# The attention mask of the last group: matmuls on TensorE, or products on VectorE and GpSimd

## The chip, the core and the metric

The kernel runs on one core of one Trainium2 chip. The metric is the device time of one launch in microseconds. Three runs of the kernel before have a median of 3718.45 us (3712.51 to 3718.55).

## What is computed

The input is 32 sequences of 256 tokens with 256 features. A gated state-space block (convolution, layernorm, a scan over the tokens, a gate) is followed by two layers of windowed attention with a feed-forward part; the result is added to the input. What matters here is the attention of one layer:

```
qkv = shift_token(x) @ wqkv                      # 8 heads of 64
q, k = l2norm, scale, rotary of q and k
sim  = q * 8 @ k^T                               # windows of 128, each with the window before it
mask = (i < j) | (i > j + WINDOW) | (j == -1)    # i: query token, j: key token
attn = softmax(where(mask, -max, sim))
x = x + (attn @ v) @ wo
...
h = layernorm(shift_token(x)) @ w1 + b1          # the feed-forward part: a * gelu(g), @ w2 + b2
```

With 256 tokens there are two windows. A key of the first window is seen by queries of the first window from its own position on, and by queries of the second window up to its own position; a key of the second window by queries of the second window from its own position on.

## The kernel before

The 32 sequences are taken in four groups of eight (`GB`, `NG`). Each group first goes through the state-space block: `group_scan` writes a list of steps by slot, 256 scan steps long (`step`, L703, on VectorE; its inputs scaled by ScalarE, L693; read out by TensorE, L715). The result of a group goes to DRAM and is loaded again, sequence by sequence, by `load_res`. The scan of group g+1 runs beside the attention of group g, so nothing is left of the scan in most of the last group.

The attention works key-major. `Attention.project` (L1137) makes q, k and v of a window (`ps_qkv`, L962); `rotated` applies the rotary tables and the norm on VectorE (L978, L983, L988, L992) and GpSimd (`rot` L986, `rn` L994, `rot` L995); `turn` transposes q and k (L1001), and ScalarE copies them (L1006).

`scores(b, kw, i0, n)` handles the keys of window `kw` for `n` head pairs from `i0` on. For the two heads of a pair it takes a bank of PSUM each, and into each bank goes first the mask: a bf16 matmul of the identity with `mask_t` (L1161), which is 0 where a key may be seen and -32768 elsewhere. The score matmuls (L1168) add to it. ScalarE takes the exponential of a bank into a tile `pT` (L1177), where the masked places become 0. A sequence has three such calls: window 1 with all four pairs, window 0 with pairs 0 and 1, window 0 with pairs 2 and 3. That is 6 mask matmuls of 128x512, 6 exponentials and 6 tiles `pT`.

`sums` adds up `pT` over the keys (`rs`, L1187), first for key window 0, heads of even number before odd, then for key window 1; VectorE inverts the sums (`rinv`, L1195). `values` multiplies with v (`ov`, L1206; copied by ScalarE, L1213). The inverse sums go through DRAM (`rb`), VectorE multiplies them on (`divide`, L1230), and `project_out` (`ps_wo`, L1012) adds the result to the residual on VectorE (L1020).

The feed-forward part has a layernorm: `normalise` transposes both windows into one bank (`tp_h`, L1249), takes their statistics (L1257, L1258, L1260), and takes the root of both windows in one GpSimd instruction (`rstd`, L1262); `apply` (L1270), `spread` (`tp_hn`, L1282, copied by ScalarE, L1288); then six times `widen` (`pa`, L1309; Gelu on ScalarE, L1317) and `product` (`ag`, L1325, on VectorE), then `narrow` (`po_f`, L1337; VectorE, L1348). In the second layer GpSimd adds the kernel's input (L1356).

The order around the change is set in two steps. A table of stages, eight to a sequence, says in which the parts of a sequence are called (`attend`, `feed`, `fetch`), and the parts of three sequences are interleaved so:

```
stage(n, 3, at.scores, b, 0, 0, 2)
stage(n, 2, at.scores, b, 1, 0, HEADS // 2)
stage(n, 5, at.scores, b, 0, 2, 2)
stage(n, 7, at.sums, b)
stage(n, 7, at.values, b)
```

From these calls a scheduler with its own costs makes the order of instructions on each engine; what is wrapped in `keep_in_program_order` it doesn't move. Each engine then works through its own list in order. DMAs of this part are issued on SyncE's queue.

Of the kernel before, what the change touches and what calls it, by code (L numbers as in the profile page):

```python
# [11 lines left out]
BF = mybir.dt.bfloat16  # L12
I32 = mybir.dt.int32
AF = mybir.ActivationFunctionType
ALU = mybir.AluOpType
# [4 lines left out]
P = 128  # L20
# [18 lines left out]
W = 128  # L39
# [13 lines left out]
def bc(ap, axis, n):  # L53

    ap = ap.unsqueeze(axis)
    shape = list(ap.shape)
    shape[axis] = n
    return ap.broadcast_to(shape)
# [15 lines left out]
def kernel(  # L74
# [29 lines left out]
    nc = tc.nc  # L104
    B = xT.shape[2]
    L = wqkv.shape[1]
    NG = B // GB

    const = ctx.enter_context(tc.tile_pool(name="const", bufs=1))
# [53 lines left out]
    for j in range(NJ):  # L163
# [13 lines left out]
    mask_t = const.tile([P, 2 * W], BF, tag="mask_t", name="mask_t")  # L177
    ident_b = const.tile([P, P], BF, tag="ident_b", name="ident_b")
# [7 lines left out]
        out=mask_t[:, W : 2 * W], in_=mask_t[:, W : 2 * W], compare_op=ALU.is_ge,  # L186
        fill=MASKED_LOW, base=0, pattern=[[-1, W]], channel_multiplier=1,
    )

    head_cols = const.tile([P, 2, 32], FP, tag="head_cols", name="head_cols")  # L190
    nc.gpsimd.memset(head_cols, 0.0)
# [27 lines left out]
    def program(ctx, exact):  # L219
# [802 lines left out]
        if exact:  # L1022

            mask = rpool.tile([P, 2 * W], FP, tag="mask", name="mask")
# [102 lines left out]
        class Attention:  # L1127

            def __init__(self, l):
                self.l = l
                self.qkv, self.rot, self.p, self.o = {}, {}, {}, {}

            def project(self, b, w, a):
                if w == 0 and a == 2:
# [16 lines left out]
            def scores(self, b, kw, i0, n):  # L1153


                qT, kT, _ = self.qkv[b]
                nq = S - kw * W
                banks = []
                for r in range(2):
                    sc = ps_w.tile([P, n, nq], FP, tag="w", name="sc")  # L1160
                    nc.tensor.matmul(  # L1161
                        sc, ident_b, bc(mask_t[:, 0:nq], 1, n), start=True, stop=False
                    )
                    banks.append(sc)
                for i in range(n):
                    for r in range(2):
                        rows = slice(r * DH, (r + 1) * DH)
                        nc.tensor.matmul(  # L1168
                            banks[r][:, i, :],
                            kT[rows, i0 + i, kw * W : (kw + 1) * W],  # L1170
                            qT[rows, i0 + i, kw * W :],
                            start=False,
                            stop=(i == n - 1),
                        )
                for r in range(2):
                    p = aw.tile([P, n, nq], FP, tag="pT", name="pT", bufs=6)
                    nc.scalar.activation(p, banks[r], AF.Exp)  # L1177
                    for i in range(n):
                        self.p[b, kw, i0 + i, r] = p[:, i, :]

            def sums(self, b):

                rs = bank(ps_w, "w", "rs")[:, 0:S]
                for kw in range(NW):
                    for r in range(2):
                        for i in range(HEADS // 2):
                            nc.tensor.matmul(  # L1187
                                rs[32 * i : 32 * i + 32, kw * W :],
                                head_cols[:, r],
                                self.p[b, kw, i, r],  # L1190
                                start=(kw == 0 and r == 0),
                                stop=(kw == NW - 1 and r == 1),
                            )
                rinv = aw.tile([P, S], FP, tag="rinv", name="rinv", bufs=1)
                nc.vector.reciprocal(rinv, rs)  # L1195
                self.rinv = rinv
# [190 lines left out]
        seqs = [(g, l, b) for g in range(NG) for l in range(L) for b in range(GB)]  # L1387
        stages = {}

        def stage(n, i, what, *args):  # L1390
            stages.setdefault(ST * n + i, []).append(partial(what, *args))

        def attend(n, at, b, nxt):

            stage(n, 0, at.turn, b, 1)
            stage(n, 3, at.scores, b, 0, 0, 2)
            stage(n, 2, at.scores, b, 1, 0, HEADS // 2)
            stage(n, 5, at.scores, b, 0, 2, 2)
            stage(n, 7, at.sums, b)
            stage(n, 7, at.values, b)  # L1400
            stage(n + 1, 0, at.put_inverse)
            stage(n + 1, 2, at.load_inverse)
            stage(n + 1, 4, at.divide, b)
            stage(n + 1, 6, at.finish, b)
            if nxt is not None:
                for w in range(NW):
                    for i, a in ((0, 2), (1, 0), (1, 1)):
                        stage(n, 3 * w + i, nxt[0].project, nxt[1], w, a)
                stage(n, 6, nxt[0].turn, nxt[1], 0)
# [22 lines left out]
            if l == L - 1 and g < NG - 1:  # L1432
                stage(n + 6, 2, load_res, g + 1, b)

        ats = [Attention(l) for _, l, _ in seqs]

        for n, (g, l, b) in enumerate(seqs):
            nxt = (ats[n + 1], seqs[n + 1][2]) if n + 1 < len(seqs) else None
            attend(n, ats[n], b, nxt)
            feed(n, g, l, b)  # L1440
# [24 lines left out]
        for t in range(max(stages) + 1):  # L1465
# [3 lines left out]
            g, r = divmod(t + 1 + group - reload, group)  # L1469
# [10 lines left out]
    with tc.If(fits > 0) as which:  # L1480
        with ExitStack() as es:
            program(es, False)
    with which.Else():
        with ExitStack() as es:
            program(es, True)
# [81 lines left out]
def _program(ins, out_shape):  # L1567
    import concourse.bacc as _bacc

    nc = _bacc.Bacc("TRN2", target_bir_lowering=False, num_devices=1)  # L1570
    arrays, args = {}, []
    for name, a in ins.items():
        arrays[f"in_{name}_dram"] = a
        args.append(
            nc.dram_tensor(
                f"in_{name}_dram", a.shape, mybir.dt.from_np(a.dtype), kind="ExternalInput"
            ).ap()
        )
    args.append(nc.dram_tensor("out_0_dram", out_shape, FP, kind="ExternalOutput").ap())
    with tile.TileContext(nc) as tc:  # L1580
        kernel(tc, *args)
    return nc, arrays
# [11 lines left out]
```

## Time and profile before

| what | before |
| --- | --- |
| median of three runs | 3718.45 us |
| the profiled execution | 3716.42 us |
| its span (first to last instruction) | 3714.5 us |
| mean granted clock of TensorE | 0.989 |
| busy: TensorE, VectorE, ScalarE, GpSimd | 3594.4, 2671.9, 2161.5, 1775.9 us |
| mask matmuls (L1161) in the whole span | 384, median 379 ns |

The page gives busy time by engine, the same in 40 slices of the span, the chain that ended last, and groups of instructions by line. PE is TensorE, PEld its weight loads, DVE is VectorE, ACT ScalarE, POOL GpSimd, SP SyncE. A row of the timeline has the start, the time to the end of the last instruction of the row, the engine and line, and in brackets the idle time of the engine before it and what ended it. An fp32 matmul stands in the trace as two instructions. Ends of matmuls are modelled, so the distance from one start to the next says more than a duration.

### The profile page before, as it was taken

The page shows a single profiled execution, that of the slowest core. Times are in us where ns is not written, and L with a number is a line of the kernel's source. Part 1 is how long each engine was busy: PE and PEld are TensorE (multiplying, and loading weights), DVE is VectorE, ACT ScalarE, POOL GpSimd, SP SyncE. Part 2 cuts the span into 40 slices and gives each one's busy share as a digit, 9 for nine tenths or more (in the row PEclk, how much of TensorE's full clock was granted, in tenths as well). Part 3 has the DMA queues.
Part 4 walks back from the last instruction along what each step waited for, and adds up shares of the span by engine and source line. Part 5 has one row for each costly group of instructions (what it writes and reads, how often), then busy time and mean ns, then how long its engine had stood idle before and what let it go on. Part 6 is the DMA issues. An engine that isn't in the chain of part 4 may idle for free.

```text
span 3714.5 us, 56989 instructions
## 1 busy us (share of the span) xinstructions
PE 3594.4 (97%) x19900; PEld 2240.4 (60%) x19900; DVE 2671.9 (72%) x5113; ACT 2161.5 (58%) x3689; POOL 1775.9 (48%) x1712
## 2 busy tenths in 40 slices
PE   7999889999999999999999999999999999999999
PEld 4444335666566566666666666666666666666666
DVE  5888889888787877887778777887776444444443
ACT  3666656666666666666666666666666444444442
POOL 4433366445455555554556555554444444433441
PEclk9999999999999999999999999999999999999999
DMA  7777655445454545445454546445453211011101
GB/s 205 203 198 203 185 164 149 130 110 135 121 140 122 150 129 150 125 112 133 110 138 124 140 138 148 126 108 137 106 135 98 60 35 50 12 35 33 30 27 36
DMA packets 469212, 435.79 MB, mean 117 GB/s; under 512 B 228835, under 2 KB 308532, under 8 KB 468788
## 3 DMA queue, kind: packets, MB, share of 16 engines
q1 hardware_dynamic: 384466, 420.05, 41.7%
q10 hardware_dynamic: 84450, 12.01, 2.1%
q8 instruction: 160, 2.62, 0.3%
q14 instruction: 136, 1.11, 0.1%
HBM read 383.70 MB, written 46.66 MB: 116 GB/s over the span
## 4 chain that ended last, share of the span: by engine, by line
PE 66%; DVE 15%; DMA 6%; POOL 5%; ACT 4%; issue 3%; SPq 0%; ACTq 0%; DVEq 0%; POOLq 0%
PE ps_qkv L962 13%; PE pa L1309 13%; PE po_f L1337 8%; DVE h L703 6%; PE y L715 5%; PE ps_wo L1012 4%; DMA xrep<-xnd 4%; PE sc L1168 4%; PE ov L1206 3%; PE ps_out L793 2%; PE ps_in L395 2%; PE tr_qk L1001 2%; ACT xrep L693 2%; DVE acc L485 2%; PE rs L1187 2%
## 5 line engine op out<-in xcount | busy, mean ns | idle before, releaser
L703 DVE CUSTOM_DVE_ANT_0 h<-h,xrep,lim 128x512 f32<-128x512 f32 x1024 | 950.2, 928 | 235.4 <-ACT xrep L693 200.8
L693 ACT ACTIVATE xrep<-xrep,beta 128x512 f32<-128x512 f32 x960 | 673.7, 719 | 342.5 <-DMA xrep<-xnd 252.5
L962 PE MATMUL ps_qkv<-qkv,res 128*128 128x512 f32 x1536 | 724.4, 607 | 18.4 <-DVE ag L1325 8.1
L1309 PE MATMUL pa<-hT,w 128*128 128x256 f32 (+1 forms) x3072 | 688.8, 386 | 1.4 <-ACT hT L1288 0.7
L1309 PEld LDWEIGHTS pa<-hT,w 128*128 128x128 f32 (+1 forms) x3072 | 492.7, 178 | 186.1 <-issue 77.4
L986 POOL TENSOR_TENSOR rot<-rot,swp 128x512 f32<-128x512 f32 x256 | 335.2, 1309 | 505.4 <-DVE swp L983 399.0
L962 PEld LDWEIGHTS ps_qkv<-qkv,res 128*128 128x128 f32 x1536 | 277.8, 191 | 327.9 <-issue 251.1
L994 POOL TENSOR_TENSOR rn<-ss,neg_half 128x8 f32<-128x8 f32 x256 | 459.2, 1794 | 15.2 <-DVE ss L992 5.2
L1325 DVE SCALAR_TENSOR_TENSOR ag<-pa,b_sb,ag 128x256 f32<-128x256 f32 (+1 forms) x448 | 213.4, 476 | 259.8 <-ACT ag L1317 257.3
L1337 PE MATMUL po_f<-ag,w 128*128 128x256 f32 (+1 forms) x1536 | 386.9, 393 | 11.6 <-DVE ag L1325 7.7
L715 PE MATMUL y<-h,ly 128*32 128x512 f32 x2048 | 356.5, 611 | 14.0 <-DVE h L703 13.1
L1337 PEld LDWEIGHTS po_f<-ag,w 128*128 128x128 f32 (+1 forms) x1536 | 272.7, 189 | 119.0 <-issue 52.0
L1262 POOL TENSOR_TENSOR rstd<-ve,neg_half 128x2 f32<-128x2 f32 x64 | 46.3, 723 | 622.3 <-DVE ve L1260 604.0
L995 POOL TENSOR_TENSOR rot<-rot,rn 128x512 f32<-128x512 f32 x256 | 292.4, 1142 | 20.1
L975 ACT ACTIVATE sq<-ps_qkv 128x512 f32<-128x512 f32 x256 | 151.9, 595 | 227.7 <-PE ps_qkv L962 175.7
L1317 ACT ACTIVATE ag<-pa,b_sb 128x256 f32<-128x256 f32 x320 | 150.2, 469 | 202.4 <-PE pa L1309 201.3
L978 DVE TENSOR_TENSOR rot<-ps_qkv,rc_sb 128x512 f32<-128x512 f32 x256 | 174.8, 683 | 82.9 <-ACT sq L975 82.2
L485 DVE SCALAR_TENSOR_TENSOR acc<-xr,wc_sb,acc 128x256 f32<-128x256 f32 x384 | 194.1, 529 | 53.7 <-POOL acc L474 53.2
L1012 PE MATMUL ps_wo<-oT,wo 128*128 128x256 f32 x1024 | 231.8, 379 | 0.2 <-ACT ag L1317 0.2
L1177 ACT ACTIVATE pT<-sc 128x512 f32<-128x512 f32 x384 | 208.5, 596 | 23.9 <-PE sc L1168 22.4
L1168 PE MATMUL sc<-qT,kT 64*128 64x128 f32 (+1 forms) x2048 | 222.0, 346 | 0.0
L1012 PEld LDWEIGHTS ps_wo<-oT,wo 128*128 128x128 f32 x1024 | 194.2, 190 | 28.3 <-ACT ag L1317 1.2
(150 smaller groups left out, 5437.0 us busy)
## 6 DMA issues: line engine op xcount, KB each, us to landing
xrep<-xnd SPq DMA_DIRECT2D x960, 256.0 KB
rb<-inv SPq DMA_DIRECT2D x128, 256.0 KB
xnd<-xn SPq DMA_DIRECT2D x64, 256.0 KB
qkv<-in_wqkv_dram SPq DMA_DIRECT2D x24, 512.0 KB
ahead<-xs_a SPq DMA_DIRECT2D x48, 256.0 KB
xp<-ahead SPq DMA_DIRECT2D x48, 256.0 KB
xd<-xnd SPq DMA_DIRECT2D x192, 64.0 KB
w<-in_w_dram SPq DMA_DIRECT2D x80, 128.0 KB
```

The source lines that it names most:

```text
L485: nc.vector.scalar_tensor_tensor(acc, xr[:, :, k : k + CH], wc_sb[:, ch, k : k + 1], acc, ALU.mult, ALU.add,)
L693: scaled = nc.scalar.activation(bx, ck[c].pop(("bx", t), bx), AF.Copy, scale=ck[c]["beta"][:, t : t + 1])
L703: nc.vector._custom_dve(TENSOR_ADD_SAT, out=h_new, in0=state["h"], in1=bx, s0=ck[c]["lim"][:, 0, t : t + 1], s1=ck[c]["lim"][:, 1, t : t + 1],
L715: nc.tensor.matmul(ck[c]["y", hb][32 * q : 32 * q + 32, :], ly[hb % 2][:, 32 * t : 32 * t + 32], ck[c].pop(("h", hb * TB + t)), start=(i = ...
L962: nc.tensor.matmul(ps, res[b][:, k, t0 : t0 + W], wt["qkv", a][:, k], start=(k == 0), stop=(k == KM - 1),)
L986: nc.gpsimd.tensor_add(rot, rot, swp)
L994: nc.gpsimd.tensor_tensor(rn, ss, neg_half, ALU.pow)
L995: nc.gpsimd.tensor_mul(rot, rot, bc(rn, 2, DH))
L1012: nc.tensor.matmul(po[:, d], wt["wo", 0][:, c, d * P : (d + 1) * P], oT[:, c, :], start=(c == 0), stop=(c == NC_ - 1),)
L1168: nc.tensor.matmul(banks[r][:, i, :], kT[rows, i0 + i, kw * W : (kw + 1) * W], qT[rows, i0 + i, kw * W :], start=False, stop=(i == n - 1),)
L1309: nc.tensor.matmul(pg if x else pa, wt["w1", m][:, k, x], self.h[:, k], start=(k == 0), stop=(k == KM - 1),)
L1337: nc.tensor.matmul(self.po[:, d], wt["w2", 0][r0 : r0 + n, m, d * P : (d + 1) * P], self.ag[m][r0 : r0 + n], start=(m == 0), stop=(m == le ...
```

## The change

In the last group (`g == NG - 1`, both layers) the mask matmuls are left out: each score matmul starts its own part of the bank, and the exponential is taken of the unmasked scores. Afterwards the tiles `pT` are multiplied in place by `mask_1`, which is 1 where a key may be seen and 0 elsewhere. GpSimd does that for the two tiles of key window 1, VectorE for the four of key window 0. `mask_1` is made once in the setup, by one GpSimd comparison of `mask_t`. The products are called at stages 3, 4 and 6 of their sequence, each a stage after its scores, and keep their place in the program's order. The other three groups are as before. The description of the change names the layernorm of both halves together as well: the diff has no line in it, and the kernel before already takes both windows together, as told above.

```diff
+    mask_1 = const.tile([P, 2 * W], BF, tag="mask_1", name="mask_1")
+    nc.gpsimd.tensor_scalar(mask_1, mask_t, -1.0, None, ALU.is_ge)
...
-            def __init__(self, l):
+            def __init__(self, g, l):
                 self.l = l
-                self.qkv, self.rot, self.p, self.o = {}, {}, {}, {}
+
+                self.apart = g == NG - 1
+                self.qkv, self.rot, self.p, self.ps, self.o = {}, {}, {}, {}, {}
...
-                    nc.tensor.matmul(
-                        sc, ident_b, bc(mask_t[:, 0:nq], 1, n), start=True, stop=False
-                    )
+                    if not self.apart:
+                        nc.tensor.matmul(
+                            sc, ident_b, bc(mask_t[:, 0:nq], 1, n), start=True, stop=False
+                        )
...
-                            start=False,
-                            stop=(i == n - 1),
+                            start=self.apart,
+                            stop=self.apart or i == n - 1,
...
                     nc.scalar.activation(p, banks[r], AF.Exp)
+                    self.ps[kw, i0, r] = p
...
+            def mask(self, kw, i0):
+
+                e = nc.gpsimd if kw else nc.vector
+                for r in range(2):
+                    p = self.ps.pop((kw, i0, r))
+                    n, nq = p.shape[1:]
+                    tc.keep_in_program_order(
+                        e.tensor_mul(p, p, bc(mask_1[:, 0:nq], 1, n))
+                    )
...
+            if at.apart:
+                for i, what in ((3, (1, 0)), (4, (0, 0)), (6, (0, 2))):
+                    stage(n, i, at.mask, *what)
...
-        ats = [Attention(l) for _, l, _ in seqs]
+        ats = [Attention(g, l) for g, l, _ in seqs]
```

## The prediction

> **What bounds the kernel now.** I read the page first (engine shares, then the 40 slices), then the table of stages, then the groups of the last stage alone, and last the timelines of TensorE, VectorE and GpSimd over one sequence of that stage.
>
> ```profile
> PE 3594.4 (97%) x19900; PEld 2240.4 (60%) x19900; DVE 2671.9 (72%) x5113; ACT 2161.5 (58%) x3689; POOL 1775.9 (48%) x1712
> ...
> PE   7999889999999999999999999999999999999999
> ...
> DVE  5888889888787877887778777887776444444443
> ```
>
> The first row is an average over different stages; the slices separate them. TensorE (PE) is full nearly everywhere, but VectorE (DVE) falls from 8 to 4 tenths for the last stretch: there the state-space scan is over and only attention and feed-forward are left. The table of stages gives it in microseconds (columns: stage, then busy time and count of PE, weight loads, DVE, ACT, POOL; then granted clock, DMA share, GB/s):
>
> ```profile
> 2400.00:2700.00 300.00, 298.36 (x1750) 190.21 (x1749) 236.66 (x450) 192.29 (x330) 148.58 (x134) 1.00 0.45 119
> ...
> 3000.00:3300.00 300.00, 300.00 (x1757) 201.37 (x1756) 131.31 (x276) 136.61 (x217) 120.89 (x97) 1.00 0.14 36
> ```
>
> In the last stage PE is busy for 300.00 of 300 us at full clock, every other engine for under half. What PE does less of there should shorten the run one for one, as long as nothing else becomes late. The last group of sequences is 16 passes through attention (8 sequences, 2 layers). Its mask products stand from 3015.26 to 3647.45 us, and these are groups of that stretch (busy us, mean ns | idle before):
>
> ```profile
> L986 POOL TENSOR_TENSOR rot<-rot,swp 128x512 f32<-128x512 f32 x60 | 76.1, 1269 | 168.8 <-DVE swp L983 118.4 <-PE sc L1161 47.3 <-PE pa L1309 3.1
> ...
> L995 POOL TENSOR_TENSOR rot<-rot,rn 128x512 f32<-128x512 f32 x60 | 62.5, 1042 | 4.7
> ...
> L1161 PE MATMUL sc<-mask_t,ident_b 128*128 128x512 bf16 x96 | 28.6, 379 | 0.0
> ...
> L1356 POOL TENSOR_TENSOR fo<-fo,xs 128x512 f32<-128x512 f32 x8 | 17.0, 2122 | 33.3 <-DVE fo L1348 23.2 <-issue 10.1
> ```
>
> All 96 mask matmuls that the change removes are there. Their mean of 379 ns is a duration with a modelled end, and neighbours overlap; what one costs is the step from start to start:
>
> ```profile
> 3303.02 3.70 PE L962 MATMUL ps_qkv<-qkv,res 128*128 128x512 f32 x8
> 3306.56 0.60 PE L1161 MATMUL sc<-mask_t,ident_b 128*128 128x512 bf16 x2
> 3307.08 1.16 PE L1168 MATMUL sc<-qT,kT 64*128 64x128 f32 x16
> ...
> 3311.16 0.66 PE L1282 MATMUL tp_hn<-ident,hn 128*128 128x128 f32 x4
> 3311.65 0.59 PE L1161 MATMUL sc<-mask_t,ident_b 128*128 128x512 bf16 x2
> 3312.17 1.14 PE L1168 MATMUL sc<-qT,kT 64*128 64x256 f32 x8
> ...
> 3324.93 0.59 PE L1161 MATMUL sc<-mask_t,ident_b 128*128 128x512 bf16 x2
> 3325.45 1.14 PE L1168 MATMUL sc<-qT,kT 64*128 64x256 f32 x8
> ...
> 3334.50 1.51 PE L1187 MATMUL rs<-pT,head_cols 128*32 128x256 f32 x32
> ```
>
> Three pairs per pass, each 0.52 us before the scores start. The row sums (rs) are the first reader of the masked probabilities; they start every 41.61 or 41.62 us, pass after pass: an in-order stream that never waits.
>
> **What the Trainium skill says.** "TensorE: Matmul & The Clock Gate", section "Back-to-back issue gap", gives N/2.4 + 2.5 ns, 216 ns for 512 columns, but a lower 131 ns for a sustained stream of load and matmul; the trace shows 260 ns (0.52/2), above both, and I use the trace. The same page, "Step-by-step", says that PE pulls a weight load ahead of running matmuls; the score loads here (187 ns median) are mostly covered so. "VectorE: DVE Perf Modes", section on the TRN2 errata, gives (N+151)/0.96 ns for an fp32 tensor_tensor: 691 ns for 512, and the trace has 686 (L978). "SBUF — State Buffer", section "Who interferes with whom": a VectorE instruction with two SBUF inputs contends with a GpSimd instruction that reads SBUF. The trace agrees: the residual add L1356, which starts beside the two-input L1230, takes 2122 ns where the add L986 of equal size takes 1269.
>
> **The change part by part.** *Removed:* 96 mask matmuls with their 96 loads of the identity. Summing the step from a pair's first start to the scores' start over the 48 pairs of the trace gives 25.16 us (0.52 or 0.53 each). Upper bound: their busy time, 28.6. Against it stands the first score load, which the identity's load (98 ns) and matmuls used to cover. Behind the qkv and pa matmuls it stays covered; behind the four short transposes at 3311.16 (0.49 us in all) up to 187 ns could show: 0 to 16 x 0.19 = 3.0 us, taken at 0, since the transposes' own loads (141 ns each) fit into their 0.12 us steps without idle. The start flags of the scores change nothing in time. PE: -25.2 us (bounds -28.6 and -22.2).
>
> *Added on GpSimd:* in each pass two products of 128x512 for the second key window. In the built order they stand behind the first window's rotation (last row L995) and ahead of the next (L986):
>
> ```profile
> 3314.26 1.04 POOL L995 TENSOR_TENSOR rot<-rot,rn 128x512 f32<-128x512 f32 x1
> 3323.86 1.27 POOL L986 TENSOR_TENSOR rot<-rot,swp 128x512 f32<-128x512 f32 x1 [8.56 <-DVE swp L983]
> ```
>
> The probabilities are there (exponentials 3308.71 to 3309.80), so the wait added is over before it begins. No row has this exact product; the nearest are 1.04 (L995, second factor spread) and 1.27 us (L986), up to 2.12 if VectorE holds it off. I take 1.27: 2.5 us into 8.56 us of idle, done near 3317.8, and first read at rs, 16 us later. Behind it wait the next rotation and, in the second layer, the residual add L1356; both still start on their VectorE inputs. Cost on the path 0; without the idle 2 x 1.27 us would delay the rotation, which the transposes need only 9 us after its end.
>
> *Added on VectorE:* four products a pass, 0.69 us each by L978 and the skill. The first two stand behind L1230 and ahead of an ag product, the other two behind L1020 and ahead of the next ag:
>
> ```profile
> 3318.45 1.22 DVE L1230 TENSOR_TENSOR oT<-oT,rb 128x1024 f32<-128x1024 f32 x1
> 3320.48 0.48 DVE L1325 SCALAR_TENSOR_TENSOR ag<-pa,b_sb,ag 128x256 f32<-128x256 f32 x1 [0.81 <-ACT ag L1317]
> ...
> 3332.00 0.69 DVE L1020 TENSOR_TENSOR res<-res,ps_wo 128x512 f32<-128x512 f32 x1 [1.70 <-PE ps_wo L1012]
> ...
> 3335.11 0.48 DVE L1325 SCALAR_TENSOR_TENSOR ag<-pa,b_sb,ag 128x256 f32<-128x256 f32 x1 [2.42 <-ACT ag L1317]
> ```
>
> First two: 1.4 us against 0.81 of idle, so ag is some 0.6 us late (up to 1.9 in the second layer, where L1356 can come between); the next VectorE row has 1.40 us of idle, and ag is read by po_f most of a pass later: cost 0. Last two: this is the tight place. L1020 ends at 3332.69, the products at 3334.1, and rs starts at 3334.50. In rs the first product's tile is read after 4 of the 16 wide matmuls and the second's after 12, at about 3334.7 and 3335.2 (16 of them in some 0.95 us), so 1.1 to 1.3 us are to spare. Dropping the pair at 3324.93 moves L1020 and rs alike. GpSimd's second rotation ends at 3331.94; it starts from VectorE work that follows two of the three pairs (-1.04 us), L1020 follows all three (-1.57 us), so the margin between that end and the products shrinks from 0.75 to 0.2 us. If one GpSimd instruction (at most 1.64 us) holds one product, rs waits about 0.5 us.
>
> *Added in the setup:* one 128x256 compare on GpSimd. Nearest row: L474, 0.55 us. GpSimd stands idle for 1.08 us there, waiting for the branch's value: 0.
>
> *Moved:* no DMA and no other instruction of the last group changes place on any queue, and no layernorm instruction anywhere. But in the first group's scan the built order differs: up to some 490 us about 105 rows on VectorE, 119 on PE, 75 on ACT, 61 on SP and 9 on GpSimd, nearly all by one to three places. PE is at 0.88 there and VectorE at 0.83, so both orders have slack and waits. 37 of the moved rows are scan steps; if each gained or lost a third of a step (mean 914 ns), that is 11 us either way. I take 0.
>
> *Sum.* The profiled execution took 3716.42 us: 3714.5 of span and 1.9 around it. Less 25.2 it gives 3691.3. The median of the runs shown is 2.0 above that execution, so the forecast against the median is 3718.45 - 25.2 = 3693.3.
>
> **The rivals.**
> *Late row sums* (the other side): the last two products each collide with a GpSimd instruction. For: L1356 shows such a hold, and the margin to the rotation is only 0.2 us. Against: it must collide twice in every pass. Price: 2 x (0.69 + 1.64) = 4.7 us where 2.5 fit (3332.69 to 3335.2), so 2.2 us in each of 16 passes, +35: 3728. It turns the gain into a loss from 1.57 us of wait a pass; one hold alone (0.5 us) gives 3701.
> *Exposed score loads:* 0.19 us at each of the 48 places, +9: 3702. Against: the covered loads above.
> *The first group's order decides:* 3704 if it loses 11 us, 3682 if it gains them. For: rows did move. Against: by few places, in a stage that no engine fills.
> *It does not do what it says:* the freed time is idle, because the stream waits elsewhere (3718). The even 41.6 us with no idle row on PE speaks against it.
>
> **How the numbers follow.** Forecast (3688 to 3698) 0.58; exposed loads or one hold (about 3702) 0.12; first group loses (3704) 0.12, gains (3682) 0.09; no gain (3718) 0.05; late row sums (3728) 0.04. The forecast lies so far from 0.2% (7.4 us, about what a measurement of this kernel can tell from no change) that faster gets 0.90, same 0.06, slower 0.04. The range reaches from 3682 to 3706: the known bounds of the removal and both signs of the first group, leaving out the last two cases and the ends of the others.
>
> **What would show it.** Right: no L1161 row after 3000 us; rs every 40.05 us; PE still without idle; the masked products at 0.7 us (DVE) and 1.0 to 1.3 (POOL). Wrong in the tight step: idle on PE before rs with DVE as its releaser. Wrong in the quiet one: the first scores of the last group come clearly before or after 3015 us. A step between 40.05 and 40.6 with no such idle means exposed loads.

## The result and the profile after

| what | before | after |
| --- | --- | --- |
| median of four runs | 3718.5 us | 3694.36 us |
| ratio of the runs, 95% interval | | 0.9932 (0.9917 to 0.9947) |
| span of the profiled execution | 3714.5 us | 3693.9 us |
| last row sums of the third group | 3001.58 us | 3001.94 us |
| step from there on, row sums to row sums | 41.61 or 41.62 us | 40.32 us |
| step to the last row sums (no projection beside it) | 30.34 us | 28.94 us |

The median fell by 24.1 us against 25.2 forecast. The interval allows 20 to 31 us, so the median can't judge the size; the steps in the profile can. The 16 passes of the last group are the 16 steps behind the third group's last row sums. The first fifteen together take 604.80 us where it was 624.22, that is -19.42; the last step gives -1.40, the start +0.36, the end another -0.1: together the 20.6 us by which the span is shorter.

The page of the changed kernel, first part and slices:

```profile
PE 3580.5 (97%) x19804; PEld 2234.3 (60%) x19804; DVE 2714.2 (73%) x5177; ACT 2163.0 (59%) x3689; POOL 1812.1 (49%) x1745
...
PE   7999989999999999999999999999999999999999
...
DVE  5888889878787777877787778877777445455553
```

96 matmuls fewer on TensorE, 64 products more on VectorE, 33 instructions more on GpSimd. VectorE rises by a tenth in some slices of the last stretch, and TensorE stays full. The table of stages says the same of the last group, and the groups of the last group show the products (busy us, mean ns):

```profile
3000.00:3300.00 300.00, 300.00 (x1759) 202.30 (x1758) 157.16 (x321) 141.64 (x223) 138.71 (x114) 1.00 0.14 37
```

```profile
L1195 DVE TENSOR_TENSOR pT<-pT,mask 128x512 f32<-128x512 f32 x64 | 49.7, 818 | 0.0
...
L1195 POOL TENSOR_TENSOR pT<-pT,mask 128x512 f32<-128x512 f32 x32 | 36.3, 1156 | 1.9 <-ACT pT L1183 1.9
```

GpSimd's product takes 1156 ns, between the two rows that bounded it. VectorE's mean of 818 is one of two cases, which the timelines tell apart. This is TensorE in one pass (start, time to the end of the row's last instruction):

```profile
3294.32 3.70 PE L965 MATMUL ps_qkv<-qkv,res 128*128 128x512 f32 x8
3297.95 1.16 PE L1174 MATMUL sc<-qT,kT 64*128 64x128 f32 x16
...
3302.02 0.66 PE L1299 MATMUL tp_hn<-ident,hn 128*128 128x128 f32 x4
3302.61 1.13 PE L1174 MATMUL sc<-qT,kT 64*128 64x256 f32 x8
...
3313.63 1.89 PE L1326 MATMUL pa<-hT,w 128*128 128x256 f32 x8
3315.45 1.13 PE L1174 MATMUL sc<-qT,kT 64*128 64x256 f32 x8
...
3324.50 1.51 PE L1204 MATMUL rs<-pT,head_cols 128*32 128x256 f32 x32
```

No mask matmul is left. But the rows ahead of the scores have become longer. From ps_qkv to the scores it is 3.63 us, where from ps_qkv to the mask it was 3.54; from tp_hn 0.59 instead of 0.49; from pa 1.82 instead of 1.73. That is 0.28 us a pass given back, about what lacks between the forecast's 1.57 and the measured 1.30. VectorE in the same pass (first layer), and one row of a pass in the second layer:

```profile
3310.05 1.29 DVE L1195 TENSOR_TENSOR pT<-pT,mask 128x512 f32<-128x512 f32 x2
...
3322.00 0.69 DVE L1023 TENSOR_TENSOR res<-res,ps_wo 128x512 f32<-128x512 f32 x1 [0.66 <-PE ps_wo L1015]
3322.61 1.29 DVE L1195 TENSOR_TENSOR pT<-pT,mask 128x512 f32<-128x512 f32 x2
...
3471.29 2.36 DVE L1195 TENSOR_TENSOR pT<-pT,mask 128x512 f32<-128x512 f32 x2
```

A pair takes 1.29 us, and the tight one, ahead of the row sums, is done at 3323.90; the row sums start at 3324.50. In the second layer the first pair, beside GpSimd's residual add (3470.32 to 3472.50), takes 2.36 us. Nothing follows from it for the row sums. GpSimd in the first of these passes:

```profile
3305.56 1.04 POOL L998 TENSOR_TENSOR rot<-rot,rn 128x512 f32<-128x512 f32 x1
3306.56 2.27 POOL L1195 TENSOR_TENSOR pT<-pT,mask 128x512 f32<-128x512 f32 x2
3314.30 1.27 POOL L989 TENSOR_TENSOR rot<-rot,swp 128x512 f32<-128x512 f32 x1 [5.46 <-DVE swp L986]
...
3321.34 1.04 POOL L998 TENSOR_TENSOR rot<-rot,rn 128x512 f32<-128x512 f32 x1
```

The two products take 2.27 us of the idle time, and 5.46 us of it remain.

### The profile page after: what moved, and what is told of

It is laid out like the page before. It is cut to its first block, busy times and chain, and to the rows that moved or that the text cites. A ratio compares the mean times of both kernels' runs of the same rounds, so it can differ in the third digit from the quotient of the medians.

```text
span 3693.9 us, 56916 instructions
## 1 busy us (share of the span) xinstructions
PE 3580.5 (97%) x19804; PEld 2234.3 (60%) x19804; DVE 2714.2 (73%) x5177; ACT 2163.0 (59%) x3689; POOL 1812.1 (49%) x1745
## 4 chain that ended last, share of the span: by engine, by line
PE 67%; DVE 15%; DMA 5%; POOL 5%; ACT 3%; issue 3%; SPq 0%; ACTq 0%; DVEq 0%; POOLq 0%
PE ps_qkv L965 13%; PE pa L1326 13%; PE po_f L1354 8%; DVE h L706 6%; PE y L718 5%; PE ps_wo L1015 4%; PE sc L1174 4%; DMA xrep<-xnd 4%; PE ov L1223 3%; PE ps_out L796 3%; PE ps_in L398 2%; PE tr_qk L1004 2%; DVE acc L488 2%; PE rs L1204 2%; ACT xrep L696 2%
```

## The experiments

Theory: the products cost nothing, TensorE is the only bound of the last group, and a pair of mask matmuls is worth 0.43 us (2 x 0.216); the other 0.09 of its 0.52 us is a gap in front of the scores that is there with and without the mask. (A step is the time from one start to the next.) Rivals: the products cost the missing 0.27 us a pass; the pair is worth 0.52 after all; the first group's new order decides. The first four kernels shared a chip, on which the kernel before had a median of 3711.29 us; for the others it was 3711.5 to 3712.5. Ratios are against before on the same chip.

| kernel | median us | ratio (95% interval) | step of the row sums, last group, us |
| --- | --- | --- | --- |
| removal alone | 3689.92 | 0.9947 (0.9928 to 0.9967) | 40.32 |
| products alone | 3708.84 | 0.9992 (0.9982 to 1.0003) | 41.61 or 41.62 |
| mask twice | 3731.47 | 1.0056 (1.0037 to 1.0076) | 42.90 or 42.91 |
| setup alone | 3709.68 | 0.9999 (0.9990 to 1.0009) | 41.61 or 41.62 |
| last pair three times | 3707.08 | 0.9986 (0.9978 to 0.9993) | 41.43 |
| all products on GpSimd | 3694.01 | 0.9961 (0.9943 to 0.9980) | 40.32 |
| all groups | 3798.71 | 1.0239 (1.0212 to 1.0266) | 40.31 to 40.33 |
| all groups, four products on GpSimd | 3812.13 | 1.0280 (1.0253 to 1.0307) | 40.32 |
| the changed kernel again | 3689.19 | 0.9927 (0.9904 to 0.9950) | 40.32 |
| first call in all groups | 3717.00 | 1.0011 (1.0002 to 1.0021) | 40.32 |
| two calls in all groups | 3719.69 | 1.0019 (1.0012 to 1.0026) | 40.32 |
| two passes more | 3683.43 | 0.9923 (0.9907 to 0.9940) | 40.32 |

**Removal alone.** The changed kernel without its products:

```diff
-            if at.apart:
-                for i, what in ((3, (1, 0)), (4, (0, 0)), (6, (0, 2))):
-                    stage(n, i, at.mask, *what)
```

> The mask matmuls of the last group are left out and the products too, so the last group's attention is unmasked (that part of the computation is missing). Theory (the products are free; what the removal doesn't bring is the 0.09 to 0.10 us with which score matmuls start after full-height matmuls, and that was inside the pair's 0.52 us): same as the changed kernel, row sums every 40.32 us, about 3694 us. Rival (the products cost the missing 0.27 us a pass): row sums every 40.05 us, about 3690 us.

The step is 40.32 us, to the hundredth that of the changed kernel: the products cost the passes nothing, and the rival falls. The median of 3689.92 against the changed kernel's 3689.19 on a later chip says the same less sharply.

**Products alone.** The mask matmuls stay in every group and the products are added:

```diff
-                    if not self.apart:
-                        nc.tensor.matmul(
+                    nc.tensor.matmul(
...
-                            start=self.apart,
-                            stop=self.apart or i == n - 1,
+                            start=False,
+                            stop=(i == n - 1),
```

> Mask matmuls kept in all groups, products added in the last one, where they multiply zeros by zero. Theory: products hidden, row sums every 41.62 us as before, about 3719 us. Rival (products cost 0.27 us a pass): 41.89 us, about 3723 us. Late row sums: idle on TensorE before the row sums with VectorE as its releaser.

The step is that of before. The two halves of the change add up: removal -1.30 us a pass, products 0.

**Mask twice.** The mask matmuls stay in every group, without products, and in the last group each stands a second time:

```diff
+                    if self.apart:
+                        nc.tensor.matmul(
+                            sc, ident_b, bc(mask_t[:, 0:nq], 1, n), start=False, stop=False
+                        )
```

> No products; in the last group each mask matmul stands twice, so four per call instead of two. Theory (a mask matmul costs 0.216 us, and 0.09 belongs to the start of the scores): the step from the first mask matmul to the scores grows from 0.52 to 0.95 us, row sums every 42.91 us, about 3739 us. Rival (the pair costs 0.52): 1.04 us, row sums every 43.18 us, about 3744 us.

One call of its scores on TensorE:

```profile
3011.72 0.38 PE L1166 MATMUL sc<-mask_t,ident_b 128*128 128x512 bf16 x1
3011.94 0.38 PE L1170 MATMUL sc<-mask_t,ident_b 128*128 128x512 bf16 x1
3012.15 0.38 PE L1166 MATMUL sc<-mask_t,ident_b 128*128 128x512 bf16 x1
3012.37 0.38 PE L1170 MATMUL sc<-mask_t,ident_b 128*128 128x512 bf16 x1
3012.68 1.16 PE L1177 MATMUL sc<-qT,kT 64*128 64x128 f32 x16
```

From mask to mask it is 0.21 to 0.22 us, from the last mask to the scores 0.31. Adding six matmuls a pass costs 1.29 us, as removing six gains 1.30. So a mask matmul is worth 0.216 us, and about 0.09 us belongs to the way into the scores. My expectation ascribed that to the change from full to half height. A row of the timeline gives the part of TensorE's array that its matmuls use, its tile (128\*128 or 64\*128). These are the last matmul of a row and the start of the next, in the kernel before:

```profile
3319.55 0.38 PE L1309 MATMUL pa<-hT,w 128*128 128x256 f32 x1
3319.77 0.59 PE L962 MATMUL ps_qkv<-qkv,res 128*128 128x512 f32 x1
...
3334.19 0.38 PE L1309 MATMUL pa<-hT,w 128*128 128x256 f32 x1
3334.50 0.42 PE L1187 MATMUL rs<-pT,head_cols 128*32 128x256 f32 x4
```

```profile
3319.55 0.19 PEld L962 LDWEIGHTS ps_qkv<-qkv,res 128*128 128x128 f32 x1
...
3334.50 0.11 PEld L1187 LDWEIGHTS rs<-pT,head_cols 128*32 128x32 f32 x1 [0.33 <-issue]
```

and in the changed kernel, ahead of the scores:

```profile
3315.14 0.38 PE L1326 MATMUL pa<-hT,w 128*128 128x256 f32 x1
3315.45 0.49 PE L1174 MATMUL sc<-qT,kT 64*128 64x256 f32 x2
```

```profile
3315.45 0.18 PEld L1174 LDWEIGHTS sc<-qT,kT 64*128 64x128 f32 x1 [0.33 <-issue]
```

From pa to ps_qkv, which has the same tile, it is 0.22 us, as from pa to pa within a row. From pa to rs and to the scores, where the tile changes, it is 0.31. The load of ps_qkv starts during the last pa; those of rs and of the scores start only with their own matmul. The length of the load doesn't decide: the longest of the three (0.19 us) leaves no gap, the shortest (0.11) does. From 3005 to 3640 us of the kernel before, every change from one line to another fits this: 0.09 us more where the tile changes, nothing more from 128\*128 to 128\*128, bf16 or fp32. The mask matmuls have the tile of the rows ahead of them, so the change to the scores' tile stays when they go. What the array does in these 0.09 us no run shows.

**Setup alone.** The kernel before, with only this in the setup:

```diff
+    mask_1 = const.tile([P, 2 * W], BF, tag="mask_1", name="mask_1")
+    nc.gpsimd.tensor_scalar(mask_1, mask_t, -1.0, None, ALU.is_ge)
```

> The kernel before with the one comparison on GpSimd in the setup, whose result nobody reads; the order in the first group is then that of the changed kernel. Theory: the first row sums of the last group start 0.4 us later, as in the changed kernel (3001.94 against 3001.58), and the time is 3719 us. Rival (the new order of the first group decides some us, either way): 3707 or 3730 us.

The time is unchanged within 0.1% (some 3.7 us). The finer expectation failed. The row sums that it calls the first of the last group are the last of the third, as the table above has them (the last group's first mask matmul starts at 3015.26 us); they stand at 2992.86 us, not at 3002. But between kernels that are equal up to there they stand anywhere from 2991.60 (removal alone) to 3001.94 (the changed kernel). The part before the last group scatters by more than such an effect, so a loss or gain of a few us there can't be told from none; one of 11 us is excluded.

**Last pair three times.** The tight step by itself, VectorE later by four products:

```diff
-                    tc.keep_in_program_order(
-                        e.tensor_mul(p, p, bc(mask_1[:, 0:nq], 1, n))
-                    )
+                    for _ in range(3 if (kw, i0) == (0, 2) else 1):
+                        tc.keep_in_program_order(
+                            e.tensor_mul(p, p, bc(mask_1[:, 0:nq], 1, n))
+                        )
```

> As the changed kernel, but VectorE makes the last two products (window 0, pairs 2 and 3) three times over, which changes no value. Theory of the tight step: the second tile is read after 12 of 16 wide row-sum matmuls, so some 1.2 us are to spare after the products; four more at 0.605 us each make the second product 1.1 us late, TensorE idles before a row-sum matmul with VectorE as releaser in each pass, row sums every 41.4 us, and of the 20 us gained 18 are lost. Rival (VectorE's products never matter to TensorE here): 40.32 us and no idle.

The step is 41.43 us, 1.11 us more, but not by the wait that I expected. TensorE and VectorE in one pass:

```profile
3206.65 1.06 PE L1205 MATMUL rs<-pT,head_cols 128*32 128x256 f32 x12
3207.64 1.95 PE L1224 MATMUL ov<-pT,v_sb 128*64 128x256 f32 x18
3209.52 1.06 PE L1205 MATMUL rs<-pT,head_cols 128*32 128x256 f32 x20
3210.51 1.51 PE L1224 MATMUL ov<-pT,v_sb 128*64 128x256 f32 x14
3211.95 1.99 PE L1327 MATMUL pa<-hT,w 128*128 128x256 f32 x8
```

```profile
3204.76 2.74 DVE L1196 TENSOR_TENSOR pT<-pT,mask 128x512 f32<-128x512 f32 x4
3207.42 0.48 DVE L1343 SCALAR_TENSOR_TENSOR ag<-pa,b_sb,ag 128x256 f32<-128x256 f32 x1
3207.82 1.41 DVE L1196 TENSOR_TENSOR pT<-pT,mask 128x512 f32<-128x512 f32 x2
```

The scheduler saw the late products and put value matmuls (ov) between the row sums, and an ag product between the masked ones. From the first row sums to pa it is 5.30 us where the changed kernel has 4.19. One wait lies hidden inside the row of twelve: its third row-sum matmul starts at 3206.96, when the first tile's third product has just ended (3206.91), 0.3 us after the second one; the changed kernel starts four within 0.02 us. The rest goes with the order: the second part of the row sums starts 0.31 us after the last ov matmul (3209.21), which is the ordinary step in front of a new tile, and 0.29 us after the last product ends (3209.23). So VectorE's products do cost TensorE time once they come later, and that rival falls. But the slack of 1.2 us was not measured; that the loss equals the 1.1 us expected from one wait is coincidence.

**All products on GpSimd.**

```diff
-                e = nc.gpsimd if kw else nc.vector
+                e = nc.gpsimd
```

> As the changed kernel, but GpSimd makes all six products of a pass: four of them (4.5 us) in the idle time of 5.5 us between the two rotations, the last two behind the second rotation, which ends 2.1 us before the row sums start. Theory: the last product ends 0.15 us after the row sums start and is read 0.7 us after, so no wait: row sums every 40.32 us in the first layer; in the second layer the input's residual add comes on top and can cost up to 0.5 us a pass (4 us in all). Rival (late row sums): GpSimd is behind in every pass, over 41 us, no gain left.

The step is 40.32 us in both layers; the only wait on a product is a single one of 0.26 us, in the last pass but one. There it parts the row sums in two, and the next step is 29.82 us where the changed kernel has 28.94:

```profile
3605.35 1.06 PE L1204 MATMUL rs<-pT,head_cols 128*32 128x256 f32 x20 [0.26 <-POOL pT L1195]
```

So in the last group it hardly matters which of the two engines multiplies.

**All groups.** If the products are free, why only the last group?

```diff
-                self.apart = g == NG - 1
+                self.apart = True
```

> The change in all four groups: 288 more mask matmuls go, 64 products a group on VectorE and 32 on GpSimd come, beside the scan. Theory (TensorE is the bound there too, at 97 to 99% busy; VectorE rises from 79 to 85%): up to 288 x 0.216 = 62 us less than the changed kernel, about 0.976 of before. Rival (VectorE's in-order queue holds up scan steps, and TensorE waits for them): no gain over the changed kernel, or a loss, 0.993 of before or more.

Slower than before by 2.4%. TensorE's three largest waits, from 600 to 2700 us of its profile (us in total, times, longest):

```profile
PE rs L1204 <- DVE pT L1195: 92.8, 32, 7.1
PE sc L1174 <- DVE ag L1342: 19.8, 13, 2.3
PE po_f L1354 <- DVE ag L1342: 7.8, 2, 5.5
```

The first is the late row sums, which were the prediction's rival for the last group. Why, one pass shows, TensorE and then VectorE:

```profile
1321.18 3.69 PE L1015 MATMUL ps_wo<-oT,wo 128*128 128x256 f32 x16
...
1327.41 0.63 PE L1204 MATMUL rs<-pT,head_cols 128*32 128x256 f32 x4
1332.91 2.56 PE L1204 MATMUL rs<-pT,head_cols 128*32 128x256 f32 x28 [4.88 <-DVE pT L1195]
```

```profile
1327.64 1.82 DVE L706 CUSTOM_DVE_ANT_0 h<-h,xrep,lim 128x512 f32<-128x512 f32 x1
...
1331.58 0.68 DVE L1023 TENSOR_TENSOR res<-res,ps_wo 128x512 f32<-128x512 f32 x1
1332.18 1.28 DVE L1195 TENSOR_TENSOR pT<-pT,mask 128x512 f32<-128x512 f32 x2
```

ps_wo is finished before 1324.9, and L1023, for which it is the input, starts at 1331.58: scan steps and convolution work stand ahead of it in VectorE's queue. In the last group L1023 starts at once, and the products with it. Two other things differ and were not separated from this: TensorE's mean granted clock is 0.976 here and 0.973 in the next kernel, where the changed kernel has 0.988 (by estimate up to 1.2% of the span, some 45 us), and the scheduler put some 1200 of VectorE's 5113 other instructions in another place.

**All groups, four products on GpSimd.** As above, and

```diff
-                e = nc.gpsimd if kw else nc.vector
+                e = nc.vector if (kw, i0) == (0, 2) else nc.gpsimd
```

> The change in all four groups, but four of a pass's six products on GpSimd (51% busy there) and only the last two on VectorE. If TensorE is the bound and VectorE the danger: as good as the variant with four on VectorE or better, 0.976 of before. If GpSimd's queue is the danger (the rotation waits behind the products): worse than that variant.

Slower still. The last pair is on VectorE here too, and the row sums wait for it for 69.8 us in the same stretch. The scores wait for 42.9 us on ag products of VectorE, against 19.8. So taking load from VectorE to GpSimd is no cure, which the next kernel looks at alone.

**First call in all groups**, with **the changed kernel again** on the same chip. The last group is unchanged; in the others only key window 1 is masked by products, on GpSimd:

```diff
-                self.apart = g == NG - 1
+                last = g == NG - 1
+                self.apart = {(1, 0), (0, 0), (0, 2)} if last else {(1, 0)}
...
+                apart = (kw, i0) in self.apart
...
-            if at.apart:
-                for i, what in ((3, (1, 0)), (4, (0, 0)), (6, (0, 2))):
-                    stage(n, i, at.mask, *what)
+            for i, what in ((3, (1, 0)), (4, (0, 0)), (6, (0, 2))):
+                if what in at.apart:
+                    stage(n, i, at.mask, *what)
```

> The changed kernel once more, on the chip of the next ones. Row sums of the last group every 40.32 us, 20.7 us less than before in the median (0.9944); the part up to the last group as in before within its scatter.

> The last group as in the changed kernel; in the groups with a scan only the two tiles of key window 1 are masked by products, on GpSimd, and window 0 keeps its mask matmuls. Theory (what made the change in all groups slow was only the last pair of products, late in VectorE's queue, and the window 1 products are read 16 us after they can be made): no wait of the row sums on a product; 48 passes x 0.43 = up to 20 us less than the changed kernel, 0.989 of before. Rival (GpSimd's added 2.3 us a pass hold up the convolution and rotation work that VectorE and TensorE wait for): no gain or a loss against the changed kernel.

The repetition came as expected. The first call in all groups lost the whole gain (3717.00 against 3689.19), so my theory of it fell: the row sums wait on a product only once, for 0.3 us, and still it is slower. From 600 to 2700 us, first of this kernel, then of the changed one on the same chip, a wait of TensorE and the groups of the convolution:

```profile
PE sc L1170 <- DVE ag L1345: 32.4, 13, 3.1
```

```profile
L488 DVE SCALAR_TENSOR_TENSOR acc<-xr,wc_sb,acc 128x256 f32<-128x256 f32 x246 | 124.9, 543 | 57.4 <-POOL acc L477 57.1
...
L477 POOL TENSOR_SCALAR acc<-xr,wc_sb,bconv_sb 128x256 f32<-128x256 f32 x82 | 70.2, 860 | 50.7 <-DVE xc L501 46.6 <-DVE pd L640 2.8 <-DVE xr L471 1.1
```

```profile
PE sc L1167 <- DVE ag L1342: 4.6, 7, 0.9
```

```profile
L488 DVE SCALAR_TENSOR_TENSOR acc<-xr,wc_sb,acc 128x256 f32<-128x256 f32 x245 | 121.7, 530 | 36.9 <-POOL acc L477 36.6
...
L477 POOL TENSOR_SCALAR acc<-xr,wc_sb,bconv_sb 128x256 f32<-128x256 f32 x81 | 58.0, 721 | 29.2 <-DVE xc L501 25.1 <-DVE xr L471 2.5 <-ACT sq L978 1.1
```

VectorE waits 57.1 instead of 36.6 us for GpSimd's convolution (acc), but GpSimd in turn waits 46.6 instead of 25.1 us for VectorE's xc, and takes 860 instead of 721 ns for its part. TensorE's scores wait 32.4 instead of 4.6 us for VectorE's ag products. So the rival's waits are there, but which of the two engines falls behind first is not shown. Nor are they separated from a different order on VectorE (some 640 of 5113 instructions in another place) and from TensorE's mean granted clock of 0.983 against 0.988.

**Two calls in all groups.** As above, with window 0, pairs 0 and 1 by products on VectorE too (`{(1, 0), (0, 0)}`):

> As the one before, and in the groups with a scan also window 0, pairs 0 and 1 by products, on VectorE; only pairs 2 and 3 keep their mask matmuls there. If only the last pair was harmful: another 20 us less, 0.984 of before. If VectorE's queue suffers from any product beside the scan: slower than the one before.

About the same as the one before (1.0019 against 1.0011), though another 96 mask matmuls are gone: their 20 us are lost as well. TensorE's largest waits are again on VectorE's ag products (24.8 us before the scores, 10.5 before the value matmuls).

**Two passes more.** The last scan step of all, which belongs to the last group and runs beside the third group's attention, ends before the third group's last two passes, so the change can start there:

```diff
-                self.apart = g == NG - 1
+                self.apart = n >= len(seqs) - L * GB - 2
...
-        ats = [Attention(g, l) for g, l, _ in seqs]
+        ats = [Attention(n, l) for n, (_, l, _) in enumerate(seqs)]
```

> The change begins two passes earlier, with the last two of the third group's second layer, beside which no scan step runs any more. Theory (the products are free wherever VectorE has no scan beside them): the row sums of two more passes follow at 40.32 us instead of 41.62, 2.6 us less than the changed kernel in the profile's steps, which a median of the runs cannot show for certain: 0.9925 of before. Rival (the tail of the scan's work still delays the products): a wait of the row sums on a product in these two passes, and no gain.

The two steps concerned are 42.04 and 40.32 us where the changed kernel has 43.34 and 41.61 or 41.62: -1.30 each, as expected. The median is the lowest of all, but against before it is 0.9923 and the changed kernel 0.9927 with wide intervals, so only the steps show the 2.6 us.

## Why the prediction was right, and where its size was off

The forecast was 3693.3 us, and 3694.36 came. The main mechanism held, and one term of the sum was mis-sized. Step by step:

- *TensorE alone bounds the last group:* right. Its part alone, removed or added, moves the step by 1.30 or 1.29 us a pass; the products as they are, and the setup, leave it.
- *-25.2 us for the matmuls:* too much. The sum took the whole step from the first mask matmul to the scores, 0.52 us. Of that 0.43 is the pair, 216 ns a matmul: the figure that the prediction had at hand and put aside for 260 (0.52/2). The other 0.09 is the gap in front of the scores' tile and stays, now behind other work. Over 48 pairs that is 4.5 us, and the profile shows 20.6. That the median's 24.1 came closer to the forecast is luck: it holds the scatter of the earlier stages.
- *The first score load stays covered, taken at 0 (bound 3.0):* this is the term that failed. I let it be exposed only behind the short transposes, since TensorE pulls loads ahead. In the trace it does so where the tile stays, and not where it changes, so 0.09 to 0.10 us shows at all three places. The prediction's own sign of it came, a step between 40.05 and 40.6 us with no idle. The rival of exposed loads had the place right and the price (0.19 each) twice too high.
- *GpSimd's products cost 0:* right, in size (2.27 us against 2.5) and place.
- *VectorE's products cost 0:* right. The pair's 1.29 us against 1.4; the margin to GpSimd's rotation is 3322.61 - 3322.38 = 0.23 us, forecast 0.2. The slack of 1.2 us was not measured: the tripled pair lost 1.11 us, but in another order of TensorE's work. The hold by the residual add came (2.36 us for the pair) and stayed hidden. The Trainium skill, "SBUF — State Buffer", section "Who interferes with whom", says that a VectorE instruction with two SBUF inputs contends with a GpSimd instruction that reads SBUF; that row agrees.
- *The setup and the first group's order, 0:* not distinguishable from 0.
- *Late row sums:* didn't happen in the last group. The mechanism is real: with the change in all groups, 2.4% slower than before, row sums that wait for VectorE's products are TensorE's largest wait (92.8 us).

## What to carry to other kernels

Here work moved off a full engine at its full price where the receiving queues were idle at that moment, and not elsewhere. Products that were free in the last group cost at least what they gained beside the scan, on either engine, though GpSimd was only about half busy there. Price a removed matmul by the step within a row, not up to whatever follows: of the pair's 0.52 us, 0.09 belonged to the change of tile behind it, which stayed, and 0.43 came.

## What was not expected of the hardware

- A bf16 matmul of 128x512 steps at 0.21 to 0.22 us in a row of four, with its own weight load each; the profile's duration is 0.38.
- In the last group each change of the array's tile costs 0.09 us, whatever the length of the load behind it (0.11 to 0.19 us). From one 128\*128 matmul to another, also from fp32 to bf16, nothing is lost.
- The passes repeat to 0.01 us from run to run and chip to chip, while the whole time of the kernel before scatters from 3700.95 to 3721.42 us on one chip: the scatter lies in the stages before the last group, not in the attention that stands alone.
